# A four-layer transformer kernel: the first stage in another order, its normalising on ScalarE, and the row transfers of layer 0 spread between products

## The chip, the cores and the metric

The kernel runs on one core of one Trainium2 chip. The metric is the device time of one execution, in microseconds. Three runs of the kernel before gave 928.27, 928.96 and 929.91 us; the median, 928.96 us, is the time before.

## What is computed

The input x is 16 batches of 128 tokens of 128 numbers, in fp32; a context tensor has 2048 rows of the same width. Four layers follow, each of two residual updates, with a gate (a tanh of one number) on each:

```
x = x + tanh(g_xattn[l]) * attention_l(layernorm(x), ctx)
x = x + tanh(g_ffn[l])   * ffn_l(layernorm(x))
```

Layer 0's attention is linear: `scores = tril(ctx ctx^T)` and the output is `Q + scores Q` with Q the normalised tokens. Its feed-forward has 8 experts of 256 hidden units, of which each token uses two:

```python
logits = flat @ Wr
topk_vals, topk_idx = top_k(logits, 2)
topk_w = softmax(topk_vals)
combine = sum(one_hot(topk_idx, 8) * topk_w[..., None], axis=1)
for e in range(8):
    y = silu(flat @ Wg[e]) * (flat @ Wu[e]) @ Wd[e]
    out = out + y * combine[:, e:e + 1]
```

Layer 1 has softmax attention and 16 experts with grouped routing and two shared experts; layer 2 has 16-head attention and a slot-based feed-forward with a GRU; layer 3 has 16-head attention at two scales, and 32 experts with one shared. The change touches layer 0 and the beginning of layer 1.

## The kernel before

Tokens are worked on in four groups of four batches, 512 tokens each; `X[g]` holds group g, tokens by features, in SBUF throughout. The names: PE is TensorE (matmuls), DVE VectorE, ACT ScalarE, POOL GpSimd, SP SyncE, which issues most DMAs. Each engine, and each DMA queue, runs its instructions strictly in the order in which a tile scheduler put them; that order comes from the order in which the Python code emits them and from their dependencies. An instruction that waits holds up all that stand behind it on the same engine.

**First stage.** `load_group` (L117) loads x and the context of a group, `load_ffn` (L144) the expert weights into one buffer `wall`. SP issues group 0, some constants, group 1, all of layer 0's weights, groups 2 and 3, then tables of rows, columns and later weights (L173 to L196). ScalarE's queue fills `xd`, 2 MB in HBM, with zeros (L212 to L217). `linear_attention(g)` (L500) transposes the context, normalises x, makes the masked scores `sm`, multiplies (`po`), and updates X[g] (L518, L519). `normed` (L249) takes means and variances on DVE, one power on POOL (`rs`, L260), and scales on DVE (`xn`, L264), four instructions of 128x128. The driver (from L1122) emits group 0's linear attention, its routing, and then groups 1 to 3 in turn. `weights_0` (L522) picks the two greatest logits and takes a softmax with an exponential (L379).

**Layer 0's experts.** `experts()` (L1028) is a generator that the driver asks for one result after the other; attention and other work is emitted between. For group 0 all 16 half-experts are computed on all tokens. One of them, called a product here, is `gated` (L440) and `down`: gate product `pg` (L445), up product `pu` (L446), SiLU `sg` on ACT (L453; in layer 1 a tanh at L450 and a DVE product at L451), `h = sg*pu` on DVE (L457), `hw = h*cb` with the token's weight, on POOL or DVE (L461), and two products later the down product, summed in `acc` (L1036). `cb` is one expert's weights of 512 tokens on all partitions, broadcast from HBM by SP (`spread`, L428). For group 0 the products from 8 on have `hw` on DVE, the others on POOL; for layer 1's group 0 it is on DVE for the products before 12.

**Groups 1 to 3 by routing.** `choose_0` (L855) is advanced at group 0's products 0, 1, 2, 4, 6, 8 and 13: normalising groups 1 to 3 into `xs`, logits and weights of all three together, counting matmuls (`counts`, L873 to L876), row numbers `to` (L897). Then POOL scatters the rows of `xs` into `xd`, sorted by expert, with 24 indirect DMAs in a row (L901). The last step makes `whose`, the expert of each block of 128 rows, and `by`, the weights of rows. `blocks_0` (L930) computes the 31 blocks of `xd` by the expert they belong to (transposes L966, products L988, weight copies `wb` L982) and writes `yd`. In the middle stands `attention_1(0)`, layer 1's attention for group 0. `return_0` (L1008) fetches each token's two rows from `yd` with indirect DMAs on POOL (L1017, eight a group, 24 in all), and adds them to X[g] with eight adds on DVE (L1024). Its steps stand at the products 0 to 12 of layer 1's first group:

```python
if (layer, g) == (1, 0):
    for i in range(BYE, NG):
        back = return_0(i)
        for k, n in enumerate(((0, 0, 2), (3, 4, 7), (8, 9, 12))[i - BYE]):
            steps.setdefault(n, []).append(("x", back, (0, i) if k == 2 else None))
```

The next group's routing is advanced at the products 9, 11, 12 and 15 there.

Of the kernel before, what the change touches and what calls it, by code (L numbers as in the profile page):

```python
# [17 lines left out]
P = 128  # L18
# [41 lines left out]
def flamingo(ctx, tc, x_in, ctx_in, mask_in, w1, w2, w3, wslot, wsmall, slots, cols_in, rows_in, consts_in,  # L60
# [48 lines left out]


    def load(name, src, dtype=F32):
        t = const.tile(list(src.shape), dtype, tag=name, name=name)
        nc.sync.dma_start(t[:], src)
        return t
# [3 lines left out]
    def load_group(g):  # L118
        xg = const.tile([P, GB, D], F32, tag=f"x{g}", name=f"x{g}")
        nc.sync.dma_start(xg[:], x_in[g * GB:(g + 1) * GB].rearrange("b s d -> s b d"))  # L120
        X.append(xg)
        cg = act.tile([P, GB, D], F32, tag="oT" if g < 2 else "qT", name="cg")
        nc.sync.dma_start(cg[:], ctx_in[g * GB:(g + 1) * GB].rearrange("b s d -> s b d"))
        C.append(cg)
# [6 lines left out]
    def weights_by_head(name, src):  # L131

        t = blank(name, [P, 4, P])
        for n in range(2):
            for s in range(2):
                o = t[:, 2 * n + s, :].rearrange("p (i x) -> p i x", i=4)
                a = src[:, n * D + 64 * s:n * D + 64 * s + 64].rearrange("p (j i d) -> p j i d", j=2, i=4)
                for j in range(2):
                    nc.sync.dma_start(o[:, :, DK * j:DK * j + DK], a[:, j])
# [32 lines left out]

    load_group(0)  # L173
    gates = load("gates", rows_in[:, 0:8].to_broadcast([P, 8]))
    wsm = load("wsmall", wsmall)
    consts = load("consts", consts_in)
    WIDE = {0: 2, 1: 4, 3: 4}
    LOADS = {0: ("0", gu0, dn0, 16, 0), 1: ("1", gu1, dn1, 18, 2), 3: ("3", gu3, dn3, 17, 1)}
    FW = {}
    load_group(1)  # L180
    FW[0], parts = load_ffn(0)
    for part in parts:
        part()
    load_group(2)
    load_group(3)
    rows = load("rows", rows_in.to_broadcast([P, NROWS]))
    cols = load("cols", cols_in)
    at = dict(offsets(CONSTS))["up"][0]
    nc.sync.dma_start(consts[P // 2:, at:at + P], consts_in[:P // 2, at:at + P])
    W1 = load("w1", w1)  # L190
    mask_i = load("mask", mask_in, I32)
    WS = load("wslot", wslot)
    SL = load("slots", slots)
    WO3 = const.tile([P, 2, D], F32, tag="wo3", name="wo3")
    for u in range(2):
        nc.sync.dma_start(WO3[u * P // 2:(u + 1) * P // 2], w3[:, 3 * D:].rearrange("(s p) d -> p s d", s=2))  # L196

    ROW, CON = offsets(ROWS), offsets(CONSTS)

    def row(name):  # L200
        at, n = ROW[name]
        return rows[:, at:at + n]

    def col(name):
        i = COLS.index(name)
        return cols[:, i:i + 1]

    def con(name):
        at, n = CON[name]
        return consts[:, at:at + n]  # L210

    vp = blank("vp", [P, GB, VB])  # L212
    xd, yd = [dram.tile([NBLK * P, D], F32, tag=n, name=n, bufs=1) for n in ("xd", "yd")]
    zeros, z0 = vp[:].rearrange("p t x -> p (t x)"), xd[:].rearrange("(p r) d -> p (r d)", p=P)
    for i in range(0, NBLK * D, GB * VB):
        n = min(GB * VB, NBLK * D - i)
        nc.scalar.dma_start(z0[:, i:i + n], zeros[:, :n])  # L217

# [14 lines left out]
    nc.gpsimd.tensor_copy(count[:], counted[:])  # L233
    tgx = const.tile([P, 4], F32, tag="tgx", name="tgx")
# [14 lines left out]
    def normed(g, xn=None):  # L249
# [11 lines left out]
        if xn is None:  # L261
            xn = act.tile([P, GB, D], F32, tag=tag_of("xn"), name="xn", bufs=1)
        for t in range(GB):
            nc.vector.tensor_scalar(xn[:, t, :], x[:, t, :], mv[:, t, 0:1], rs[:, t:t + 1], ALU.subtract, ALU.mult)  # L264
# [75 lines left out]
    def first(v, n, k):  # L340
# [10 lines left out]
        sel = small.tile([P, nt, n], F32, tag=tag_of("sel"), name="sel", bufs=2 if side[0] == "x" else 1)  # L351
# [59 lines left out]
    def spread(comb, ne, width):  # L411
# [12 lines left out]
        for e in range(ne // n):  # L424
            cb = bcast.tile([P, GT], F32, tag="cb", name="cb")
            for i in range(n):
                k = P // n
                nc.sync.dma_start(cb[i * k:(i + 1) * k], by[i, e:e + 1].to_broadcast([k, GT]))  # L428
# [11 lines left out]
    def gated(chain, w, xnT, cb, tanh, banks, vector):  # L440
# [13 lines left out]
        if cb is None and tanh:  # L454
            nc.vector.scalar_tensor_tensor(h[:], sg[:], 0.5, pu[:], ALU.mult, ALU.mult)
        else:
            nc.vector.tensor_tensor(h[:], sg[:], pu[:], ALU.mult)  # L457
# [3 lines left out]
        (nc.vector if vector else nc.gpsimd).tensor_tensor(hw[:], h[:], cb[:], ALU.mult)  # L461
# [38 lines left out]
    def linear_attention(g):  # L500
        pt = tr_tile()
# [5 lines left out]
        xn = normed(g)  # L507
# [5 lines left out]
        nc.vector.tensor_tensor(sm[:], ps, bc(tri[:], 1, GB), ALU.mult)  # L513
        po = split(acc_tile())
        for t in range(GB):
            mm(po[:, t, :], sm[:, t, :], xn[:, t, :])
        y = work.tile([P, GB, D], F32, tag="se", name="y0")
        nc.vector.tensor_tensor(y[:], po, xn[:], ALU.add)  # L518
        add_gated(g, y[:], tgx[:, 0:1])  # L519


    def weights_0(p):  # L522
# [3 lines left out]
        sel, m8 = first(more, 8, 2)  # L526
        return sel, softmax_selected(l, m8[:, :, 0], sel, 8, "0")
# [306 lines left out]

    def with_tanh(layer, g):
# [3 lines left out]
    def routing(layer, g):  # L839

        xn = normed(g)
# [3 lines left out]
        comb = weights_0(logits_of(xnT, wsm[:, 0:8], 8))[1] if layer == 0 else weights_1(xnT) if layer == 1 else weights_3(xnT, with_tanh(layer, g))  # L845
# [9 lines left out]
    def choose_0():  # L855

        xs = act.tile([P, NT, D], F32, tag="kTm", name="xs", bufs=1)
        groups = range(BYE, NG)
        for i, g in enumerate(groups):
            normed(g, xs[:, i * GB:(i + 1) * GB])  # L860
            yield
        p = bank("logits")[:, :NT * 8].rearrange("p (t e) -> p t e", e=8)
        for i, g in enumerate(groups):
            xT = transposed(xs[:, i * GB:(i + 1) * GB], "a0", act, None)
            for t in range(GB):
                mm(p[:, i * GB + t, :], xT[:, t * P:(t + 1) * P], wsm[:, 0:8])
        yield
        sel, comb = weights_0(p)
# [8 lines left out]
        yield  # L877
# [19 lines left out]
        nc.vector.tensor_scalar(to[:], two[:, 0:2, :], -1.0, None, ALU.add)  # L897

        for t in range(NT):
            for k in range(2):  # L900
                apart("xd", nc.gpsimd.indirect_dma_start(  # L901
                    out=xd[:], out_offset=bass.IndirectOffsetOnAxis(ap=to[:, k, t:t + 1], axis=0), in_=xs[:, t, :],
                    in_offset=None))
        yield
# [18 lines left out]
        yield  # L923
# [84 lines left out]
    def return_0(g):  # L1008

        to, by, _ = places[0]  # L1010
        ys = []
        for k, tag in enumerate(("xns", "xnTs")):
            y = act.tile([P, GB, D], F32, tag=tag, name="y0", bufs=1)
            ys.append(y)
            for t in range(GB):
                i = (g - BYE) * GB + t
                apart(f"y{g}{k}", nc.gpsimd.indirect_dma_start(  # L1017
                    out=y[:, t, :], out_offset=None, in_=yd[:],
                    in_offset=bass.IndirectOffsetOnAxis(ap=to[:, k, i:i + 1], axis=0)))
            yield  # L1020
        for k, y in enumerate(ys):
            for t in range(GB):
                i = (g - BYE) * GB + t
                nc.vector.scalar_tensor_tensor(X[g][:, t, :], y[:, t, :], by[:, k, i:i + 1], X[g][:, t, :], ALU.mult,  # L1024
                                               ALU.add)
        yield

    def experts():  # L1028
# [23 lines left out]
        for at, (layer, g) in enumerate(ORDER):  # L1052
# [10 lines left out]
            if moving:  # L1063
                nxt = choose_0()
# [270 lines left out]
```

## Time and profile before

| | |
|---|---|
| median of three runs | 928.96 us |
| the profiled execution | 930.84 us |
| its span | 929.1 us |
| mean granted TensorE clock | 0.965 |
| busy: PE, DVE, ACT, POOL | 834.3, 580.6, 259.3, 282.6 us |
| `hw` on POOL, 128x512 | 126 times, mean 1278 ns |
| `h` on DVE, 128x512 | mean 683 ns |
| `xn` on DVE, 128x128 | mean 399 ns |
| gather on POOL | 24 times, mean 987 ns |

A row of a timeline or a group has the start, the busy time, the engine, the line, the operation, `out<-in` by the program's names, and in brackets how long the engine stood idle ahead of it and which instruction ended the wait ("issue" where the profile shows none). PEld is TensorE's weight load, which runs beside PE. A matmul in fp32 shows as two. The granted clock is the share of full speed at which TensorE was allowed to run. In the slices each digit is the busy share in tenths of one fortieth of the span. The profiled execution lasted 1.7 us longer than its span.

### The profile page before, as it was taken

What the parts mean: (1) busy time and instruction counts of PE and PEld (TensorE: products, weight loads), DVE (VectorE), ACT (ScalarE), POOL (GpSimd) and SP (SyncE); (2) the same over time, 40 slices, a digit from 0 to 9 for tenths busy, and PEclk for the clock granted to TensorE, in tenths of its full rate; (3) what the DMA queues carried; (4) which work ended last, traced back from release to release, by engine and by line L of the source; (5) the groups of instructions that cost most, each with busy time, mean ns of one, the idle gap of its engine ahead of it and who ended that gap; (6) DMA issues with size and microseconds to landing.
All of it is one profiled execution on the core that took longest, in us unless ns stands there. A gap on an engine that the chain in (4) does not pass through costs nothing.

```text
span 929.1 us, 16015 instructions
## 1 busy us (share of the span) xinstructions
PE 834.3 (90%) x6183; PEld 468.5 (50%) x6183; DVE 580.6 (62%) x1628; ACT 259.3 (28%) x457; POOL 282.6 (30%) x283
## 2 busy tenths in 40 slices
PE   3889399877999999999899999999989998999997
PEld 3554289534544554455455555555554554554443
DVE  4756252566977475666675866677666668566622
ACT  1222166221321222232223222223222232322321
POOL 3326521353233124311421113421114223313443
PEclk9979699978999999999999999999999999999999
DMA  9711212552121012100202112310002111211231
GB/s 305 211 17 40 64 46 79 159 162 63 24 69 44 27 35 80 46 21 28 69 35 67 35 47 62 123 37 24 24 24 72 35 48 46 76 51 49 94 103 34
DMA packets 55677, 62.12 MB, mean 67 GB/s; under 512 B 14312, under 2 KB 33512, under 8 KB 55472
## 3 DMA queue, kind: packets, MB, share of 16 engines
q1 hardware_dynamic: 53776, 55.90, 19.9%
q0 software_dynamic: 1536, 3.15, 1.1%
q10 hardware_dynamic: 288, 2.03, 0.6%
q8 instruction: 49, 0.80, 0.4%
q14 instruction: 28, 0.23, 0.1%
HBM read 53.97 MB, written 7.09 MB: 66 GB/s over the span
## 4 chain that ended last, share of the span: by engine, by line
PE 54%; DVE 21%; POOL 8%; issue 8%; ACT 4%; DMA 2%; another core or an unknown queue 1%; SPq 1%; POOLq 0%; DVEq 0%; ACTq 0%
PE mm L108 8%; PE acc L1036 7%; PE pg L445 7%; PE pu L446 7%; POOL hw L461 3%; DVE sg L451 3%; PE mm L593 2%; PE po L487 2%; DVE h L457 2%; DVE mp L481 2%; POOL rs L260 2%; POOL y L1017 2%; DVE xn L264 2%; PE tr L244 2%; PE po L490 2%
## 5 line engine op out<-in xcount | busy, mean ns | idle before, releaser
L461 POOL TENSOR_TENSOR hw<-h,cb 128x512 f32<-128x512 f32 x126 | 161.0, 1278 | 459.4 <-DVE h L457 348.1
L446 PE MATMUL pu<-xnTx,wall 128*128 128x512 f32 x288 | 156.4, 626 | 14.9 <-DVE sg L451 13.1
L1036 PE MATMUL acc<-hw,wall 128*128 128x512 f32 x288 | 153.9, 618 | 10.6 <-DVE h L457 9.9
L445 PE MATMUL pg<-xnTx,wall 128*128 128x512 f32 x288 | 154.8, 620 | 7.8 <-issue 4.7
L450 ACT ACTIVATE sg<-pg 128x512 f32<-128x512 f32 x123 | 73.6, 598 | 244.7 <-PE pg L445 230.5
L457 DVE TENSOR_TENSOR h<-sg,pu 128x512 f32<-128x512 f32 x145 | 99.1, 683 | 60.9 <-PE pu L446 40.7
L451 DVE SCALAR_TENSOR_TENSOR sg<-sg,pg 128x512 f32<-128x512 f32 x123 | 83.6, 680 | 51.4 <-ACT sg L450 51.3
L1036 PEld LDWEIGHTS acc<-hw,wall 128*128 128x128 f32 x288 | 55.1, 198 | 71.3 <-issue 53.0
L446 PEld LDWEIGHTS pu<-xnTx,wall 128*128 128x128 f32 x288 | 52.4, 197 | 75.9 <-issue 39.1
L481 DVE TENSOR_REDUCE mp<-mm 128x4 f32<-128x512 f32 (+1 forms) x112 | 65.8, 645 | 21.1 <-PE mm L593 19.9
L445 PEld LDWEIGHTS pg<-xnTx,wall 128*128 128x128 f32 x288 | 50.1, 194 | 50.2 <-issue 35.1
L495 DVE RECIPROCAL rcw<-po 128x128 f32<-128x128 f32 (+1 forms) x28 | 25.2, 900 | 57.1 <-PE po L490 44.8
L264 DVE TENSOR_SCALAR xn<-x,mv,rs 128x128 f32<-128x128 f32 x116 | 40.3, 399 | 25.4 <-POOL rs L260 25.4
L615 ACT ACTIVATE pts<-mm 128x512 f32<-128x512 f32 x64 | 33.6, 602 | 73.3 <-PE mm L609 73.3
L487 PE MATMUL po<-pts,vp 128*32 128x128 f32 (+1 forms) x896 | 46.1, 274 | 7.6 <-ACT pts L615 6.7
L260 POOL TENSOR_TENSOR rs<-ve,neghalf 128x4 f32<-128x4 f32 x32 | 33.2, 1037 | 61.8 <-DVE ve L258 61.7
L490 PE MATMUL po<-pts,own 128*32 128x128 f32 (+1 forms) x896 | 44.3, 266 | 0.5 <-issue 0.5
L453 ACT ACTIVATE sg<-pg 128x512 f32<-128x512 f32 x33 | 19.7, 597 | 67.9 <-PE pg L445 58.4
L487 PEld LDWEIGHTS po<-pts,vp 128*32 128x32 f32 (+1 forms) x896 | 21.3, 108 | 29.9 <-ACT pts L615 14.0
L254 DVE BATCH_NORM_STATS2 st<-x 128x6 f32<-128x128 f32 x128 | 29.5, 280 | 10.2 <-DMA x<-in_x 9.9
L593 PE MATMUL mm<-kTm,qT 32*128 32x256 f32 x256 | 30.5, 413 | 0.0
L1017 POOL DMA_INDIRECT y<-yd,to x24 | 23.7, 987 | 21.7 <-DMA yd<-yb 8.8
(335 smaller groups left out, 1226.0 us busy)
## 6 DMA issues: line engine op xcount, KB each, us to landing
cb<-combD SPq DMA_DIRECT2D x72, 256.0 KB
cb<-combD SPq DMA_DIRECT2D x128, 128.0 KB
wall<-in_gu SPq DMA_DIRECT2D x24, 256.0 KB
wall<-in_dn SPq DMA_DIRECT2D x12, 256.0 KB
xb<-xd SPq DMA_DIRECT2D x7, 256.0 KB
yd<-yb SPq DMA_DIRECT2D x7, 256.0 KB
xd<-vp ACTq DMA_DIRECT2D x1, 1072.0 KB
x<-in_x SPq DMA_DIRECT2D x4, 256.0 KB
```

The costliest lines, as they stand in the source:

```text
L108: nc.tensor.matmul(out=o, lhsT=l, rhs=r, start=start, stop=stop)
L264: nc.vector.tensor_scalar(xn[:, t, :], x[:, t, :], mv[:, t, 0:1], rs[:, t:t + 1], ALU.subtract, ALU.mult)
L445: in_turn(chain, nc.tensor.matmul(out=pg[:], lhsT=w[:, 0], rhs=xnT[:], start=True, stop=True))
L446: in_turn(chain, nc.tensor.matmul(out=pu[:], lhsT=w[:, 1], rhs=xnT[:], start=True, stop=True))
L450: nc.scalar.activation(sg[:], pg[:], AF.Tanh, scale=0.5)
L451: nc.vector.scalar_tensor_tensor(sg[:], sg[:], 1.0, pg[:], ALU.add, ALU.mult)
L457: nc.vector.tensor_tensor(h[:], sg[:], pu[:], ALU.mult)
L461: (nc.vector if vector else nc.gpsimd).tensor_tensor(hw[:], h[:], cb[:], ALU.mult)
L481: nc.vector.tensor_reduce(mp[:, 0:n, 32 * i + 16:32 * i + 18], src, AX.X, ALU.max)
L487: in_turn(chain, nc.tensor.matmul(out=po[32 * jj:32 * jj + 32, 0, :], lhsT=vcols, rhs=pts, start=first, stop=last, skip_group_check=True))
L490: in_turn(chain, nc.tensor.matmul(out=po[32 * jj:32 * jj + 32, 1, :], lhsT=own[rows, r, :], rhs=pts, start=False, stop=last, skip_group_ch ...
L1036: in_turn(chain, nc.tensor.matmul(out=acc[0][:], lhsT=w[:, 2], rhs=h[:], start=n == 0, stop=last))
```

## The change

The loads come in another order: context 0 on ScalarE's queue, all of x and the context ahead of most weights, the zero fill of `xd` behind them on SP's queue, and the tables of later layers behind the broadcasts of `cb`. The first stage is emitted by a list, `FIRST`, with the linear attention, group 0's routing ("r") and the choosing of groups 1 to 3 ("c1" to "c3") as generators. Layer 0 normalises on ScalarE. The sum `po + xn` is made by a matmul with the identity. The weights of the two chosen experts come from a tanh; logits and weights are made group by group, and `places_0` then counts over all. The scatters are spread over the products 6 to 15 (one or two each, the rest after the last), each behind the latest `hw` on POOL; the gathers over the products 0 to 17 of layer 1's group 0 and the first two of group 1, in turn from both lists, with two more buffers; the adds come at product 6 (group 1), 14 (group 2) and product 4 of the next group (group 3). In layer 0's group 0, `hw` is on DVE at the even products from 6 on, in layer 1's group 0 at those before 4. The next routing there is advanced at 12, 14, 15 and 17. `attention_1(0)` is emitted after group 0's experts end, as before, but TensorE's order now has its head (transposes to scores) ahead of the first block.

The diff, cut to its core:

```diff
-        nc.sync.dma_start(cg[:], ctx_in[g * GB:(g + 1) * GB].rearrange("b s d -> s b d"))
+        (nc.sync if g else nc.scalar).dma_start(cg[:], ctx_in[g * GB:(g + 1) * GB].rearrange("b s d -> s b d"))
...
+    load_group(1)
+    FW[0], parts = load_ffn(0)
+    parts[0]()
+    load_group(2)
+    load_group(3)
+    for part in parts[1:]:
+        part()
+    consts = load("consts", consts_in)
+    xd, yd = [dram.tile([NBLK * P, D], F32, tag=n, name=n, bufs=1) for n in ("xd", "yd")]
...
+        nc.sync.dma_start(z0[:, i:i + n], zeros[:, :n])
...
-        for t in range(GB):
-            nc.vector.tensor_scalar(xn[:, t, :], x[:, t, :], mv[:, t, 0:1], rs[:, t:t + 1], ALU.subtract, ALU.mult)
+        if on_act:
+            off = small.tile([P, GB], F32, tag="off", name="off")
+            nc.gpsimd.tensor_tensor(off[:], mv[:, :, 0], rs[:], ALU.mult)
+            nc.gpsimd.tensor_scalar(off[:], off[:], -1.0, None, ALU.mult)
+        for t in range(GB):
+            if on_act:
+                nc.scalar.activation(xn[:, t, :], x[:, t, :], AF.Identity, bias=off[:, t:t + 1], scale=rs[:, t:t + 1])
...
-        y = work.tile([P, GB, D], F32, tag="se", name="y0")
-        nc.vector.tensor_tensor(y[:], po, xn[:], ALU.add)
-        add_gated(g, y[:], tgx[:, 0:1])
+        in_turn(chain, nc.tensor.matmul(out=po, lhsT=ident[:], rhs=xn[:], start=True, stop=False, skip_group_check=True))
...
+        add_gated(g, po, tgx[:, 0:1])
...
-        return sel, softmax_selected(l, m8[:, :, 0], sel, 8, "0")
+        nc.vector.tensor_tensor(mid[:], m8[:, :, 0], m8[:, :, 1], ALU.add)
...
+        nc.scalar.activation(e[:], e[:], AF.Tanh)
...
+    SEND = [(n, 1 + (n + 1) % 2) for n in range(6, 16)]
+    FETCH = {0: [(n, 2) for n in range(4)] + [(n, 1) for n in range(4, 18)], 1: [(0, 1), (1, 1)]}
+    ADD = {0: [(6, 1), (14, 2)], 1: [(4, 3)]}
+
+    def on_vector(layer, g, n):
+
+        return (layer, g) == (0, BYE - 1) and n > 5 and n % 2 == 0 or (layer, g) == (1, 0) and n < 4
...
         for t in range(NT):
             for k in range(2):
-                apart("xd", nc.gpsimd.indirect_dma_start(
+                yield
+                ins = nc.gpsimd.indirect_dma_start(
                     out=xd[:], out_offset=bass.IndirectOffsetOnAxis(ap=to[:, k, t:t + 1], axis=0), in_=xs[:, t, :],
-                    in_offset=None))
-        yield
+                    in_offset=None)
+                apart("xd", ins)
+                behind_of("hw", ins)
...
+            tags = ("ya", "yb") if (g - BYE) % 2 else ("xns", "xnTs")
...
+                        if not t and not k:
+                            behind_of("h", ins)
...
+                    apart(f"y{g}{k}", ins)
+                    behind_of("hw", ins)
+                    yield
...
-                for n in (9, 11, 12, 15) if (layer, g) == (1, 0) else (3, 7, 8, 13):
+                for n in (12, 14, 15, 17) if (layer, g) == (1, 0) else (3, 7, 8, 13):
...
+    FIRST = [0, 0, 1, 0, 1, "r", 1, "r", 2, 2, "c1", "r", 2, "r", "c1", 3, 3, "c2", "c1", 3, "c2", "c3", "c2", "c3", "c3"]
...
+    first_of = {g: linear_attention(g) for g in range(NG)}
+    first_of["r"] = routing(0, 0)
+    first_of.update({f"c{g}": choose_0(g) for g in range(BYE, NG)})
+    for name in FIRST:
+        side[0] = "x" if name == "r" else "m"
+        next(first_of[name])
     side[0] = "m"
-    for g in range(1, NG):
-        linear_attention(g)
+    latest["spread"] = latest["cb"]
+    rows = load("rows", rows_in.to_broadcast([P, NROWS]))
...
+    sending, fetching = places_0(), return_0()
+    next(sending)
```

`behind_of("hw", ins)` orders an instruction behind the latest `hw` on POOL at that point of the emission, without a wait on another engine; `behind_of("spread", ins)` does so for the broadcasts of `cb`. The two softmax weights are written as half of one plus or minus the tanh of half their difference: `e = tanh(l - (top1 + top2)/2)`, then `0.5*e + 0.5`, times the selection.

## The prediction

> **What bounds the kernel now.** I read the page's slices first, then a table of windows, then the timelines of GpSimd and VectorE in the two stretches where TensorE stands still. In the slices (23.2 us each) TensorE is the bound nearly everywhere, but for the first slice, the fifth (93 to 116 us) and the eighth to tenth (163 to 232 us):
>
> ```profile
> PE   3889399877999999999899999999989998999997
> PEclk9979699978999999999999999999999999999999
> ```
>
> The windows give sizes. Columns: the stretch, its length, then busy time of PE, PEld, DVE, ACT and POOL with counts, the granted clock, the DMA share and GB/s.
>
> ```profile
> 90.00:100.00 10.00, 3.91 (x10) 1.41 (x8) 1.38 (x2) 0.60 (x1) 7.66 (x8) 0.95 0.16 52
> 100.00:110.00 10.00, 2.79 (x6) 1.23 (x7) 1.38 (x2) 0.58 (x1) 5.55 (x7) 0.50 0.21 63
> 112.00:170.00 58.00, 57.24 (x460) 54.10 (x461) 25.25 (x82) 32.86 (x61) 11.36 (x18) 0.97 0.21 59
> ...
> 180.00:184.00 4.00, 0.00 (x0) 0.00 (x0) 1.80 (x5) 0.60 (x1) 3.09 (x4) 1.00 0.54 193
> 184.00:200.00 16.00, 9.79 (x13) 3.61 (x14) 7.69 (x25) 0.60 (x1) 12.06 (x12) 0.61 0.70 208
> ...
> 213.00:217.60 4.60, 0.00 (x0) 0.00 (x0) 1.53 (x4) 0.13 (x1) 3.39 (x6) 0.71 0.20 53
> ...
> 226.00:287.00 61.00, 57.30 (x221) 30.49 (x220) 50.52 (x167) 18.54 (x32) 18.22 (x18) 1.00 0.17 50
> ```
>
> Between 112 and 170 TensorE is full, and after 226 nearly so; what is won at 90 to 110 or at 180 to 218 therefore passes on to the end. The cause of both holes is GpSimd's queue. First the scatters, 24 of them, one each 1.26 us (0.96 and 0.30 of issue), once the row numbers `to` are there (DVE line):
>
> ```profile
> 74.15 0.16 DVE L897 TENSOR_SCALAR to<-two 128x24 int32<-128x24 f32 x1
> ```
>
> ```profile
> 74.62 1.23 POOL L901 DMA_INDIRECT xd<-xs,to  x1 [1.72 <-DVE rank_in L915]
> 76.15 0.96 POOL L901 DMA_INDIRECT xd<-xs,to  x1 [0.30 <-issue]
> ...
> 103.93 0.95 POOL L901 DMA_INDIRECT xd<-xs,to  x1 [0.30 <-issue]
> 104.88 1.73 POOL L982 COPY wb<-wall 128x512 f32 x3
> 112.66 1.04 POOL L260 TENSOR_TENSOR rs<-ve,neghalf 128x4 f32<-128x4 f32 x1 [6.05 <-DVE ve L258]
> ```
>
> The blocks' first product starts at 111.92. Then the gathers of layer 1's first group, from 175.99 to 214, at the same 1.25 us. Behind each stands a VectorE add (L1024), and behind the adds in VectorE's own order the gating products `h`:
>
> ```profile
> 182.20 0.35 DVE L1024 SCALAR_TENSOR_TENSOR x<-y,by,x 128x128 f32<-128x128 f32 x1 [5.21 <-DMA y<-yd,to]
> ...
> 191.98 0.66 DVE L457 TENSOR_TENSOR h<-sg,pu 128x512 f32<-128x512 f32 x1
> ...
> 216.07 0.35 DVE L264 TENSOR_SCALAR xn<-x,mv,rs 128x128 f32<-128x128 f32 x1 [5.09 <-POOL rs L260]
> ```
>
> VectorE's `h` of product 3 is ready to run near 182 and runs at 191.98, since eight adds with late data stand ahead of it; `xn` waits at 216 for an `rs` that GpSimd holds behind eight gathers. From 170 to 287 TensorE idles 19.1 us (0.01, 4.00, 6.21, 0.51, 4.60, 0.06 and 3.70 by the windows), and the half clock after each hole costs some 5.9 more (9.79 busy x 0.39 lacking = 3.8, and from 217.6 to 226 8.34 x 0.25 = 2.1). That is all there is to win there, about 25 us.
>
> **Part by part, first stage.** Removed: the xd fill and constants ahead of the inputs, so x1 lands near 6 instead of 10.8 (VectorE's wait for it ended at 10.80) and group 1 is updated near 21.7 instead of 28.5; four adds of 0.69 us on VectorE; two exponential table loads of 1.28. Added: 4 matmuls with the identity (0.86 each warm), 16 normalising activations instead of VectorE's 0.34 each, two tiny GpSimd operations a group. No row shows a scalar activation of 128x128 with two pointers; a 128x256 exponential takes 0.384 and a 128x512 with a pointer bias 0.687, so I take 0.4 to 0.5 each, 1.65 for four against 1.1 on VectorE. ScalarE is 28% busy, so this lies under other work except in group 0's own chain, which also gets the two GpSimd operations: its normalised tokens come about 4 us later (26.8 against 22.7), but without the reduce, reciprocal and table load the first product is at about 32.5 against 30.51. If that cover fails the start is up to 2 us later still.
>
> The counting matmuls start at 67.14 now and `to` follows 7.0 later. In the new order they stand behind the products 4, not 7: three products fewer, 3 x 2.57 = 7.7, and the other groups' first stage is some 6.8 ahead. So 32.5 + (67.1 - 30.5) - 7.7 - 6.8 = 54.6, and `to` at about 62 (60 to 64). By then product 5's hw (1.28 by the row of 126, mean 1278) stands ahead of the scatters, so they begin near 64.
>
> **Scatters between products.** From there GpSimd's order holds 24 scatters x 1.26 = 30.3, five hw x 1.28 = 6.4, and two weight copies x 0.61 = 1.2: 37.9 together, ending near 102 against 104.9. Two products take TensorE 2 x 2.57 = 5.14, and GpSimd one hw and three scatters, 1.28 + 3.78 = 5.06: neither waits long for the other. TensorE ends group 0's products near 88, and ten scatters remain behind. In the new order attention 1's head for group 0 comes ahead of the first block, and its `rs` stands behind the last scatter: 102 + 1.0 (rs) + 1.1 (xn) + 1.05 (transposes) + 0.6 (copy) = 105.7, then two projections at half clock 3.8, 0.7 for the bias copy, two warm 2.1, values and scores 2.0, block transposes and copy 1.7: first block product near 116. Before it is at 111.92, but the head's 6.65 us (transposes from 115.08, projections to scores from 117.29 to 122.89) and 1.2 of half clock come later, so the same point is 119.8. Gain 4. It can be 9 if `to` comes at 58, and -4 if it comes near 70. Two long unexplained waits lie under the train now (ScalarE 7.72 before 97.44, VectorE 9.80 before 102.34). If such waits fall between products in the new order, they cost 0 to 8; I take 0, since ten scatters still end last.
>
> Here a rule speaks against the change. The Trainium skill, "SBUF — State Buffer", section "A bandwidth-pool intuition that's wrong (but worth ruling out)", says that a GpSimd-issued DMA that takes about 620 ns alone takes about 3100 ns while VectorE holds the shared port. The row says otherwise: the scatters take 0.96 both from 80 to 92, with VectorE's products running, and from 93 to 102, with VectorE idle. By the row the 14 scatters that now lie between products cost nothing more; by the rule each waits at least for one 0.68 us product, 14 x 0.68 = 9.5, and the stage gains -5.5 instead of 4. I take the row, since those products are the same instructions.
>
> **Gathers between products.** Now 8 gathers in one run and all eight adds ahead of `h` of product 3. In the new order eight gathers still lead, but group 1's adds are taken singly between the products 2 and 6, and each further gather has a hw of product n in front of it. GpSimd then needs 1.28 + 1.26 = 2.54 per product, TensorE 2.57. Landing 5 us after issue as now, `h` of product 3 runs near 184, of 4 near 187, of 5 near 191.4, of 6 near 197 (208.85 now). VectorE loses eight hw of 0.68 to GpSimd, which is where the slack comes from; what is late next is GpSimd itself, with `rs` (1.05) and the row add (1.26) between hw and gather. Walking on to the scores of attention 1, group 1, the same counts of products put them at 209.3 instead of 221.2: gain 11 or 12, I take 11. Bounds: 5 if the `rs` still waits for a full train, 18 if nearly all the idle and cold time of 25 goes. Routing of layer 1's next group ends three products later, with its broadcasts issued at the last product. The row for this is the stage's own start at 170, where routing also ended last and TensorE was busy 9.99 of 10 us: I take 0, with 3 as the other end. Later loads (layers 2 and 3) are moved behind the broadcasts into a time with a DMA share of 0.2: nothing.
>
> **Sum.** 930.84 for the profiled execution (span 929.1, 1.7 around it), less 4 and 11: 915.8. The median of the three runs, 928.96, lies 1.9 under the profiled one: 914.0.
>
> **The rivals.**
> - A, as above: 914, own range 908 to 921. For it: both holes follow one queue, and the rates of GpSimd and TensorE match. Chance 0.52.
> - B, nearly all stalls go: stage one gains 9 (`to` at 58), stage two 18: 902. For it: the idle and cold time is there. Against: GpSimd has no slack at 2.54 of 2.57. Chance 0.17.
> - C, GpSimd stays the bound: stage one gains nothing, as hw and weight copies stretch the train by 7.6 and eat the earlier start, and the gathers gain 5: 924. For it: GpSimd carries more work in both stages. Chance 0.17.
> - D, slower: the scatter train in GpSimd's in-order queue. It is 37.9 long instead of 30.3, so all rests on an earlier `to`. It decides at `to` near 66: later than that, the stage loses. If the reordered first stage gains nothing (`to` at 74.15), the train ends at 114, the stage loses 8, the gathers give 5 back: 932. For it: group 0's first product starts later, and three routings of 12 small VectorE operations replace one. Against: counts stand three products earlier in TensorE's order. Chance 0.14. That the change does nothing is not likely: the order of all five engines differs.
>
> About 0.2% (1.9 us) is what a measurement of this kernel can tell from no change. Faster by more: A, B and most of C, 0.82; within: a part of C, 0.04; slower: D, 0.14. The range takes in B and C, from 901 to 928; D and gains over 28 stay out.
>
> **What would show it.** `to` at 60 to 64 with scatters ending near 102, each still 0.96; the first block product near 116, with attention 1's head before it; no hole at 180 to 184 or 213 to 217 (less 4 us); `h` of product 3 within 2 us of its up-projection. Wrong would be: scatters or gathers over 1.3 us in length beside VectorE's products, `to` after 66, GpSimd full and TensorE waiting for hw from product 4 on in layer 1, or a new wait at the start of layer 1's second group.

## The result, and the profile after

The changed kernel takes 922.61 us (median of 5 runs, 919.22 to 924.82) against 928.96: a ratio of 0.9931, 95% interval 0.9905 to 0.9956. That is 6 us faster where 15 was forecast. Measured again, on another chip, it was 921.37 against 930.46, 9 us, a ratio of 0.9909 (0.9883 to 0.9936). The profiled execution, 919.22 us with a span of 917.5, is the fastest of the five; times inside it are read for where stalls lie, not for a us of the total.

TensorE's slices on the page:

```profile
PE   5897599889879999999999999999989999999997
```

The fifth slice still has a hole (5 for 3), the ninth and tenth are fuller (8 and 9 for 7 and 7), but the eleventh fell from 9 to 8 and the twelfth from 9 to 7. The row numbers and the scatters, from the timelines of VectorE and GpSimd:

```profile
56.65 0.16 DVE L935 TENSOR_SCALAR to<-two 128x24 int32<-128x24 f32 x1
```

```profile
59.51 1.28 POOL L941 DMA_INDIRECT xd<-xs,to  x1 [0.19 <-DMA w2h<-in_w]
...
64.21 1.27 POOL L470 TENSOR_TENSOR hw<-h,cb 128x512 f32<-128x512 f32 x1 [1.98 <-DVE h L462]
65.63 1.01 POOL L941 DMA_INDIRECT xd<-xs,to  x1 [0.15 <-issue]
...
98.32 0.97 POOL L941 DMA_INDIRECT xd<-xs,to  x1 [0.31 <-issue]
99.31 1.06 POOL L257 TENSOR_TENSOR rs<-ve,neghalf 128x4 f32<-128x4 f32 x1
```

TensorE's timeline has the hole behind the scatters, and the first block product:

```profile
101.17 1.15 PE L241 MATMUL tr<-ident,xn 128*128 128x128 f32 x4 [11.77 <-DVE xn L268]
...
111.33 1.16 PE L1034 MATMUL pg<-xbT,wb 128*128 128x128 f32 x8 [0.68 <-ACT xbT L1014]
```

The row numbers come 17.5 us earlier, the scatters end 5.6 earlier, and the first block product starts 0.6 earlier, with attention 1's head for group 0 already done. The first gather then starts at 166.18, 9.8 us before 175.99. From there on hardly anything more is gained. A point that both kernels share is the copy of the last expert sum of layer 1's second group, from which on TensorE's order is all but the same in both. Before, and then after:

```profile
369.33 0.59 ACT L1039 COPY yT<-acc 128x512 f32<-128x512 f32 x1 [1.16 <-PE acc L1036]
```

```profile
359.03 0.58 ACT L1092 COPY yT<-acc 128x512 f32<-128x512 f32 x1 [1.16 <-PE acc L1089]
```

That is 10.3 us earlier, where the first gather was 9.8 earlier.

How that comes about is seen when both are cut into stretches of 50 us from the first gather. First the kernel before:

```profile
176.00:226.00 50.00, 34.62 (x89) 15.83 (x88) 27.78 (x76) 10.01 (x15) 29.00 (x31) 0.80 0.46 135
226.00:276.00 50.00, 46.98 (x192) 25.89 (x192) 41.96 (x146) 15.38 (x27) 14.11 (x14) 1.00 0.18 53
276.00:326.00 50.00, 47.52 (x438) 23.96 (x436) 30.16 (x56) 11.26 (x21) 9.85 (x8) 1.00 0.11 34
```

The changed kernel:

```profile
166.20:216.20 50.00, 41.64 (x119) 19.56 (x118) 28.43 (x74) 11.90 (x19) 29.70 (x29) 0.90 0.48 148
216.20:266.20 50.00, 41.36 (x138) 20.28 (x138) 38.00 (x123) 12.23 (x21) 22.89 (x23) 0.97 0.16 50
266.20:316.20 50.00, 46.40 (x277) 24.01 (x275) 40.24 (x112) 11.42 (x21) 17.06 (x17) 1.00 0.14 43
```

TensorE's busy time (first column after the length) rises by 7.0 us in the first stretch, falls by 5.6 in the second and by 1.1 in the third. The clock, 0.80 to 0.90 and 1.00 to 0.97, says the same. The gain of the first stretch is given back 50 us later. Where, VectorE's timeline shows:

```profile
190.10 0.68 DVE L462 TENSOR_TENSOR h<-sg,pu 128x512 f32<-128x512 f32 x1
191.20 0.50 DVE L1064 SCALAR_TENSOR_TENSOR x<-y,by,x 128x128 f32<-128x128 f32 x1 [0.41 <-DMA y<-yd,to]
...
196.38 0.35 DVE L1064 SCALAR_TENSOR_TENSOR x<-y,by,x 128x128 f32<-128x128 f32 x1 [3.29 <-DMA y<-yd,to]
...
200.22 0.35 DVE L1064 SCALAR_TENSOR_TENSOR x<-y,by,x 128x128 f32<-128x128 f32 x1 [2.95 <-DMA y<-yd,to]
...
225.53 0.67 DVE L462 TENSOR_TENSOR h<-sg,pu 128x512 f32<-128x512 f32 x1
226.12 0.34 DVE L1064 SCALAR_TENSOR_TENSOR x<-y,by,x 128x128 f32<-128x128 f32 x1
...
250.10 0.35 DVE L1064 SCALAR_TENSOR_TENSOR x<-y,by,x 128x128 f32<-128x128 f32 x1 [2.26 <-DMA y<-yd,to]
...
254.45 0.35 DVE L1064 SCALAR_TENSOR_TENSOR x<-y,by,x 128x128 f32<-128x128 f32 x1 [1.47 <-DMA y<-yd,to]
254.72 0.68 DVE L578 TENSOR_TENSOR aT<-po,qT 128x512 f32<-128x512 f32 x1
```

The adds at 191.20, 196.38, 200.22, 250.10 and 254.45 each wait for a row, and VectorE's other work stands behind them. TensorE's own timeline has the holes that follow, 3.16 us behind `sg` after the add at 200.22 and 4.74 behind `aT` after the one at 254.45:

```profile
204.53 1.80 PE L451 MATMUL pu<-xnTx,wall 128*128 128x512 f32 x2 [3.16 <-DVE sg L456]
...
255.45 1.57 PE L108 MATMUL mm<-w,aT 128*128 128x128 f32 x8 [4.74 <-DVE aT L578]
```

From 60 to 300 us, VectorE's waits for rows are 19.8 us in ten, against 9.7 in three before. The last gather starts at 248.86, where before it was 214.01.

These adds do not stand where the change meant them. Of each group's eight adds only the first is ordered behind the latest `h` (in the kernel, `if not t and not k: behind_of("h", ins)`), and the second follows it, since both update the same tokens. For group 2 these two ran at 226.12 and 226.50, behind `h` of product 14 (225.53), as meant. The six others ran from 191.20 to 221.81, the first of them right behind `h` of product 7 (190.10). Of the 19.8 us of waits 16.3 fall on such adds of groups 2 and 3.

### The profile page after: what moved, and what is told of

The parts are those of the page before. It is cut to its first block, busy times and chain, and to the rows that moved or that the text cites. A ratio compares the mean times of both kernels' runs of the same rounds, so it can differ in the third digit from the quotient of the medians.

```text
span 917.5 us, 16089 instructions
## 1 busy us (share of the span) xinstructions
PE 831.0 (91%) x6191; PEld 464.1 (51%) x6191; DVE 571.5 (62%) x1598; ACT 266.3 (29%) x484; POOL 302.0 (33%) x312
## 4 chain that ended last, share of the span: by engine, by line
PE 48%; DVE 20%; POOL 13%; issue 9%; DMA 5%; ACT 4%; POOLq 0%; SPq 0%; DVEq 0%; ACTq 0%
PE mm L108 8%; POOL hw L470 6%; PE acc L1089 6%; PE pg L450 6%; PE pu L451 5%; DVE mp L490 3%; DVE sg L456 3%; PE mm L617 2%; PE po L496 2%; POOL xd L941 2%; DVE h L462 2%; DMA y<-yd,to 2%; POOL rs L257 2%; PE po L499 2%; PE mm L612 2%
## 5 line engine op out<-in xcount | busy, mean ns | idle before, releaser
L470 POOL TENSOR_TENSOR hw<-h,cb 128x512 f32<-128x512 f32 x137 | 176.2, 1287 | 443.5 <-DVE h L462 353.7
L451 PE MATMUL pu<-xnTx,wall 128*128 128x512 f32 x288 | 154.4, 618 | 10.5 <-DVE sg L456 9.0
L451 PEld LDWEIGHTS pu<-xnTx,wall 128*128 128x128 f32 x288 | 51.9, 194 | 72.5 <-issue 39.8
L268 DVE TENSOR_SCALAR xn<-x,mv,rs 128x128 f32<-128x128 f32 x96 | 33.1, 402 | 24.1 <-POOL rs L257 24.1
L241 PE MATMUL tr<-ident,xn 128*128 128x128 f32 x100 | 22.4, 310 | 19.2 <-DVE xn L268 17.0
L496 PEld LDWEIGHTS po<-pts,vp 128*32 128x32 f32 (+1 forms) x896 | 21.4, 108 | 30.3 <-ACT pts L639 14.8
L241 PEld LDWEIGHTS tr<-ident,xn 128*128 128x128 f32 x100 | 12.6, 142 | 35.9 <-issue 14.6
```

Of the source, the lines that this page charges most:

```text
L451: in_turn(chain, nc.tensor.matmul(out=pu[:], lhsT=w[:, 1], rhs=xnT[:], start=True, stop=True))
L470: latest["hw"] = nc.gpsimd.tensor_tensor(hw[:], h[:], cb[:], ALU.mult).ins
L496: in_turn(chain, nc.tensor.matmul(out=po[32 * jj:32 * jj + 32, 0, :], lhsT=vcols, rhs=pts, start=first, stop=last, skip_group_check=True))
```

## The experiments

Times are medians, ratios are against the kernel before on the same chip. Where two experiments ran on different chips, a difference of 1 or 2 us between them says little. The changed kernel itself once more, on the chip on which three of the others ran (no adds, plain first stage, scatters in one run with the gathers of before):

> The changed kernel as it is, beside the other three on one chip. Both theories: within 2 us of its first measurement, 920 to 925; it is the base for the three others of this call.

921.37 us, ratio 0.9909 (0.9883 to 0.9936). As expected.

**Which part gained.** The gathers put back as before, in the changed kernel:

```diff
-        return (layer, g) == (0, BYE - 1) and n > 5 and n % 2 == 0 or (layer, g) == (1, 0) and n < 4
+        return (layer, g) == (0, BYE - 1) and n > 5 and n % 2 == 0 or (layer, g) == (1, 0) and n < 12
...
-                for n in (12, 14, 15, 17) if (layer, g) == (1, 0) else (3, 7, 8, 13):
+                for n in (9, 11, 12, 15) if (layer, g) == (1, 0) else (3, 7, 8, 13):
...
-                for n, k in FETCH.get(g, ()):
-                    steps.setdefault(n, []).extend([("x", fetching, None)] * k)
...
+                    back = return_0(i)
+                    for k, n in enumerate(((0, 0, 2), (3, 4, 7), (8, 9, 12))[i - BYE]):
```

(and `return_0` as it was)

> The changed kernel with layer 0's gathers, adds, weightings and routing steps in layer 1's first group put back as before: only the first stage and the scatters are changed. Theory (the first stage and scatters give all, the spread gathers give nothing): first gather near 166, as in the changed kernel, and 921 to 925 us, no slower than the changed kernel by over 2. Rival (the gathers gave part of it and something later took it): 926 to 929.

920.32 us, ratio 0.9913 (0.9881 to 0.9946), first gather at 168.12. With the adds in place, the first stage and the scatters give all of the gain. The mirror, the kernel before with only that part changed:

> The kernel before with only the gathers, adds, weightings and routing steps of layer 1's first group spread as in the change. Theory: 927 to 931 us, no gain, since each add waits in VectorE's queue for a row that a weighting on GpSimd holds back. Rival (my forecast of 11 us for this part): 916 to 920.

931.95 us, ratio 1.0032 (1.0012 to 1.0052). My 11 us for this part are refuted; alone it costs 3.

**The first stage.** Scatters in one run:

```diff
-    SEND = [(n, 1 + (n + 1) % 2) for n in range(6, 16)]
+    SEND = [(6, 2 * NT)]
...
-        return (layer, g) == (0, BYE - 1) and n > 5 and n % 2 == 0 or (layer, g) == (1, 0) and n < 4
+        return (layer, g) == (0, BYE - 1) and n > 5 or (layer, g) == (1, 0) and n < 4
...
-                behind_of("hw", ins)
```

> The changed kernel, but all 24 scatters in one run after product 6 and the weightings of all products after 5 on VectorE: GpSimd has nothing between the scatters. Theory (the earlier row numbers are what gained; the spreading only lengthens the train, 37.9 instead of 30.3 us): the last scatter near 90 instead of 99, first block product near 102 instead of 111, and 912 to 916 us. Rival (spreading the scatters is what gains, because a run of scatters holds TensorE up): 925 or more.

915.18 us, ratio 0.9857 (0.9829 to 0.9884), 6 to 7 us faster than the changed kernel. GpSimd's and TensorE's timelines of this run:

```profile
58.76 1.22 POOL L941 DMA_INDIRECT xd<-xs,to  x1 [4.17 <-DVE to L935]
...
89.74 0.96 POOL L941 DMA_INDIRECT xd<-xs,to  x1 [0.30 <-issue]
```

```profile
94.92 1.11 PE L1011 MATMUL tr<-ident,xb 128*128 128x128 f32 x4 [6.53 <-DMA xb<-xd]
96.71 2.08 PE L1033 MATMUL pg<-xbT,wb 128*128 128x128 f32 x8 [0.68 <-ACT xbT L1013]
```

The last scatter starts at 89.74 instead of 98.32, since only one weighting (at 61.42) still stands among the scatters. TensorE ends group 0's products at about the same time as in the changed kernel, and its hole is 6.53 us instead of 11.77. The first block comes even before the 102 expected, since in this order it stands ahead of attention 1's head. So of the change's two ideas for the scatters, row numbers early is the one that gains, and spreading them between weightings takes a part of it away. What the other place of attention 1's head adds was not tried apart. Normalising back on VectorE:

```diff
-        normed(g, xs[:, own], on_act=True)
+        normed(g, xs[:, own])
```

(and the same in `routing` and `linear_attention`)

> The changed kernel with layer 0's normalising back on VectorE, everything else as changed. Theory (the order of the first stage gained, and the move to ScalarE is nearly neutral, since group 0's own chain gets longer by two GpSimd operations and a slower scale): row numbers within 2 us of 58 and 920 to 925 us. Rival (ScalarE's share is what brings the row numbers forward): row numbers after 62 and 926 or more.

924.05 us, ratio 0.9955 (0.9936 to 0.9974), row numbers at 58.93. The traces that keep the changed kernel's first stage up to there have them at 56.65 to 58.51, so ScalarE brings them forward by 2 us at most. Of the time it gives some 1 to 4 us, hardly clear of noise, as the intervals overlap. And the list `FIRST` in a plain order:

```diff
-    FIRST = [0, 0, 1, 0, 1, "r", 1, "r", 2, 2, "c1", "r", 2, "r", "c1", 3, 3, "c2", "c1", 3, "c2", "c3", "c2", "c3", "c3"]
+    FIRST = [0] * 3 + ["r"] * 4 + [1] * 3 + [2] * 3 + [3] * 3 + ["c1"] * 3 + ["c2"] * 3 + ["c3"] * 3
```

> The changed kernel with its hand-written order of the first stage put back to a plain one: group 0's linear attention and routing, then the groups 1, 2, 3, then their choices; loads, ScalarE's normalising and the tanh weights stay. Theory (the earlier row numbers come from the counts standing three products earlier and from the loads, not from the interleaving): row numbers at 55 to 61, within 3 us of the changed kernel. Rival (the interleaving is what gains): row numbers after 64 and 926 or more.

924.28 us, ratio 0.9947 (0.9924 to 0.997), row numbers at 59.64, 1.4 later than in the changed kernel on the same chip (58.20). So most of the 17.5 us by which the row numbers come earlier are left even in the plain order, and the time is 2.9 us more than the changed kernel's, as the theory had it. Whether the loads or the counts' place in TensorE's order bring them was not tried apart.

**What holds the second half.** The 24 adds left out of the changed kernel (groups 1 to 3 then lack layer 0's experts):

```diff
-                for t in range(GB):
+                for t in range(0):
                     for k, y in enumerate(ys):
                         ins = nc.vector.scalar_tensor_tensor(X[g][:, t, :], y[:, t, :], by[:, k, t0 + t:t0 + t + 1],
```

> The changed kernel with the 24 adds of the fetched rows left out; the gathers stay, but nothing reads their rows, so groups 1 to 3 go on without layer 0's experts. Theory (late rows ahead of VectorE's other work are what TensorE still waits for in layer 1's first group): the 20 us of waits and 8 us of adds leave VectorE, and 905 to 913 us. Rival (that stretch is held by VectorE's and GpSimd's other work, weightings, routing and norms, and the rows only decide where the holes lie): 917 to 922.

901.66 us, ratio 0.9704 (0.9674 to 0.9734), 19.7 less than the changed kernel on the same chip and more than expected. The 50 us from its first gather on:

```profile
168.20:218.20 50.00, 49.21 (x158) 23.65 (x157) 35.96 (x82) 16.07 (x25) 37.28 (x36) 1.00 0.50 157
```

With the same gathers and weightings on GpSimd, which is even busier (37.28 us against 29.70), TensorE is full at 49.21 of 50. GpSimd's pace was not the bound; the adds were. The run takes away three things together: VectorE's waits for rows, the adds' own 8 us, and the wait of attention 1 for their sums. The kernel before with its adds left out in the same way:

> The kernel before with the 24 adds of the fetched rows left out, gathers as they were, so groups 1 to 3 go on without layer 0's experts. Theory (the return of the rows costs the same in both kernels, the change only moves its stalls): some 20 us less than before, 907 to 912, as with the changed kernel. Rival (the change did shorten the return, and something else took the gain): 25 us or more less, under 905.

920.67 us, ratio 0.9901 (0.9866 to 0.9937): only 8.3 less. Neither number of the expectation holds; the adds cost much more in the changed kernel. What is left before without adds is one large hole in TensorE's timeline:

```profile
208.12 1.02 PE L108 MATMUL tr<-cols,perm 128*128 128x4 f32 x4 [12.34 <-POOL perm L1165]
```

`perm` is made on GpSimd behind the train of gathers. So spreading the gathers does take this block away: without adds the two kernels are 18 to 19 us apart (ratios 0.9704 and 0.9901, medians 901.66 and 920.67), of which the first stage is about 8, and 10 to 11 are left for the spread gathers (with the weightings and the routing that moved with them), about what was forecast. With the adds, which cost 8.3 before and 19.7 after, they are gone.

Adds later, each behind the latest `h`:

```diff
-    ADD = {0: [(6, 1), (14, 2)], 1: [(4, 3)]}
+    ADD = {0: [(8, 1), (16, 2)], 1: [(5, 3)]}
...
-                        if not t and not k:
-                            behind_of("h", ins)
+                        behind_of("h", ins)
```

> The changed kernel with the three sets of adds two products later, the last one product later (8, 16 and 5 instead of 6, 14 and 4), and each add ordered behind the latest h, so that their rows have landed. Theory (single adds with late rows in VectorE's queue took the gain): waits of adds for rows fall from 14 us to under 5, and 915 to 919 us. Rival (GpSimd itself, with a weighting ahead of every gather, is the bound): 921 to 925.

918.89 us, ratio 0.9896 (0.9864 to 0.9928). With every add held to its product, the waits for rows are gone altogether. Yet only 1 to 4 us are won, not 20, and the intervals overlap, so late rows alone are not what the adds cost. TensorE has other holes now, among them 4.39 us at 237.50 for `comb`, the routing of the next group. Eight adds, 231.39 to 235.87, now stand within its chain of small operations on VectorE. Hence two runs with the routing put forward again, as before the change:

```diff
-                for n in (12, 14, 15, 17) if (layer, g) == (1, 0) else (3, 7, 8, 13):
+                for n in (9, 11, 12, 15) if (layer, g) == (1, 0) else (3, 7, 8, 13):
```

in the changed kernel,

> The changed kernel with one number list put back: the next group's routing in layer 1's first group is advanced at the products 9, 11, 12 and 15 instead of 12, 14, 15 and 17. Theory (in the changed kernel the second half of layer 1's first group is held by group 3's late rows, not by the routing): within 2 us of the changed kernel, 920 to 925. Rival (the later routing gave the gain back): 915 to 918.

928.69 us, ratio 1.0015 (1.0001 to 1.0029), and with the later adds,

> The kernel with the later adds, and with the routing at the products 9, 11, 12 and 15 as before. Theory (with the rows' waits gone, the late routing is what TensorE waits for next, 4.4 us before the transpose of comb): that wait goes, and 912 to 917 us against 918.9 without. Rival (VectorE's chain is the bound whatever its order): 918 to 921.

927.1 us, ratio 0.9984 (0.9963 to 1.0005). Both expectations and both rivals were wrong: an earlier routing costs 6 to 10 us (928.69 against 921.37 to 922.61, or by the ratios 1.0015 against 0.9909 to 0.9931; 927.1 against 918.89), and with the later adds the wait for `comb` stays (3.82 at 241.03). From the first gather to the copy of the shared point it takes 200.2 and 200.6 us instead of 192.9. With the rows spread over 80 us, the late routing is not a price of the change but a need. The rows fetched in one run and asked for late:

```diff
-    FETCH = {0: [(n, 2) for n in range(4)] + [(n, 1) for n in range(4, 18)], 1: [(0, 1), (1, 1)]}
-    ADD = {0: [(6, 1), (14, 2)], 1: [(4, 3)]}
+    FETCH = {0: [(0, 16), (8, 8)]}
+    ADD = {0: [(7, 1), (12, 2), (16, 3)]}
...
-        return (layer, g) == (0, BYE - 1) and n > 5 and n % 2 == 0 or (layer, g) == (1, 0) and n < 4
+        return (layer, g) == (0, BYE - 1) and n > 5 and n % 2 == 0 or (layer, g) == (1, 0) and n < 12
...
-                        if not t and not k:
-                            behind_of("h", ins)
+                        behind_of("h", ins)
...
-                    behind_of("hw", ins)
```

> The changed kernel with gathers in one run from the start of layer 1's first group (16, then 8 when buffers are free), not behind any weighting, the weightings of its products before 12 on VectorE, and the adds at the products 7, 12 and 16, each behind the latest h: rows come early and are asked for late. Theory (the pace of the weightings makes group 3's rows late, and VectorE waits for them): last gather before 212 instead of 249, no wait for rows, 910 to 916 us. Rival (VectorE with twelve weightings more than it can hide): 919 to 924.

921.91 us, ratio 0.9927 (0.9898 to 0.9956). The last gather starts at 198.84, the adds wait 0.3 us for rows in all, and nothing is won. GpSimd's timeline of this run, and TensorE's, show what is late in their place:

```profile
193.96 0.94 POOL L1071 DMA_INDIRECT y<-yd,to  x1 [0.30 <-issue]
194.92 1.04 POOL L257 TENSOR_TENSOR rs<-ve,neghalf 128x4 f32<-128x4 f32 x1
```

```profile
196.40 0.48 PE L241 MATMUL tr<-ident,xn 128*128 128x128 f32 x1 [5.61 <-DVE xn L268]
...
252.40 0.38 PE L421 MATMUL tr<-ident,comb 128*16 128x128 f32 x1 [4.92 <-DVE comb L378]
```

The `rs` of attention 1 stands behind the gathers again, as in the kernel before, and `comb` comes late out of VectorE's chain. So neither side of the expectation holds: it is not late rows alone, and not VectorE's weightings alone.

**Together.** Four combinations with the scatters in one run, each with edits shown above. With adds later and routing earlier:

> Three edits together: scatters in one run with the weightings of the products after 5 on VectorE, adds later and each behind the latest h, routing at 9, 11, 12 and 15. If the two stages are independent, the gains add: 7 from the scatters, 3 to 8 from the others, 907 to 912 us. If the first stage's gain is partly taken back in the second, as the changed kernel's was not by this one: 913 to 916.

914.85 us, ratio 0.9875 (0.9845 to 0.9905), no better than the scatters' edit alone (nor does it settle whether the stages add, since the earlier routing has its own cost). With the gathers as before:

> Scatters in one run with the weightings of the products after 5 on VectorE, and gathers, adds, weightings and routing of layer 1's first group as before. Theory (spread gathers neither gain nor lose): 913 to 917 us, as with spread gathers, 915.2. Rival (spread gathers gain some us once the first stage is short): 918 to 921.

917.36 us, ratio 0.9868 (0.9843 to 0.9892): as with spread gathers (0.9857), the intervals overlap. With the rows early and the adds late:

> The same with the scatters in one run and the weightings after product 5 of layer 0 on VectorE. If the two stages are independent, 6 us less than the kernel with rows early and adds late alone, 904 to 910 if that gained, 913 to 918 if not.

914.41 us, ratio 0.9844 (0.9816 to 0.9873), 7.5 less than without the scatters' edit: that edit's gain adds on. Finally adds later with the routing left late:

> Scatters in one run with the weightings after product 5 of layer 0 on VectorE, and the later adds (products 8, 16 and 5), routing as changed. If the gains of the two edits add: 6 to 7 less than the kernel with the later adds (918.9), 911 to 913 us. If the second stage gives the later adds' gain back: 914 to 916, as with the scatters' edit alone.

909.26 us, ratio 0.9776 (0.9753 to 0.98), 13 us faster than the changed kernel as first measured. It is the best of the versions that keep the adds, 2 us better than the lower case expected.

## Why the prediction was wrong

The sign was right, and the mechanism of the first stage. The total, 15, was more than twice the 6 us measured first (9 in the second measurement), and the split between the stages was nearly the reverse: 4 and 11 forecast, about 8 to 10 and 0 measured.

**First stage, 4 forecast.** `to` was put at 62 and came at 56.65: the first product ran at 31.50 instead of 32.5, the counts at 51.07 instead of 54.6, and `to` followed 5.6 later instead of 7.0. The train was put at 37.9 and took 39.8 (59.51 to 99.31), so its end was 99.3, not 102. From there to the first block product I allowed 14 us and it took 12.0. In these two terms the sum was off by 2.7 and 2.0, and with them the first block product is at 111.33 instead of 116. The point of before that I compared with, 119.8, was put together by hand; the next point that both kernels share in full, the first gather, is 9.8 us earlier. What I had as rival B's share for this stage, 9, was the right size. GpSimd kept pace with TensorE, as the rates 5.06 and 5.14 said, but that the train would still be shorter without the weightings, I had in my sum (30.3 against 37.9) and did not follow: it is probably most of the 6 to 7 us of the scatters' edit. The 16 normalising activations of the sum were 32 in the kernel, since routing and choosing normalise too.

The rule on the shared port did not bear on this case. The passage is about a `tensor_copy` on VectorE, and VectorE's products under the scatters are `tensor_tensor`, so the -5.5 worked out from it had no ground. The tile views of `xd`, of before and then of the changed kernel (minimum, median and maximum in ns):

```profile
L901 POOL DMA_INDIRECT xd<-xs,to x24: 954/958/1226, 74.6 to 103.9; - x24
```

```profile
L941 POOL DMA_INDIRECT xd<-xs,to x24: 954/969/1277, 59.5 to 98.3; - x24
```

The row was the right one: 11 ns more at the median, not 680.

The two unexplained waits under the train, taken at 0, did not come back as holes of that size: TensorE's last group-0 sums ran at 86.71, against 88 in the sum. Nor do they count in the old first stage: in the two other traces that have it, the last of these sums ran at 95.0 and 95.4 instead of 104.8, and the first block at 112.7 all the same.

**Second stage, 11 forecast: the step that failed** is "Walking on to the scores of attention 1, group 1, the same counts of products put them at 209.3 instead of 221.2: gain 11 or 12". The walk has group 1's adds in it and puts those of groups 2 and 3 at nothing, without a reason. To product 6 it holds: shifted by the 9.8 us of the first stage, `h` of the products 3, 4 and 5 ran at 185.2, 187.8 and 191.6, where I put 184, 187 and 191.4, and `h` of product 6 at 194.5, even before my 197. Behind product 7 stand six adds of group 2, and the waits of the first three, 6.65 us together, hold VectorE. The point compared, the transpose of the attention's weights, before and then after:

```profile
221.24 0.87 PE L298 MATMUL tr<-ident,sm 128*128 128x128 f32 x4
```

```profile
207.83 0.81 PE L302 MATMUL tr<-ident,sm 128*128 128x128 f32 x4
```

Shifted, 207.83 is 217.6, 8.3 later than the 209.3 forecast: a gain of 3.6, not 11 or 12. Nor are the counts of products the same there: TensorE has begun nine before and eleven after. Two products are some 5.1 us of its time, so that by my estimate about 8.7 us were in hand at this point. Then I let the gain pass on to the end, because TensorE was nearly full after 226 before the change. But before, all rows had been fetched by 214. In the changed kernel the rows of groups 2 and 3 come until 249, VectorE waits for them, and the 7.0 us of the first 50 us are taken back by 5.6 and 1.1 in the next hundred. I had named as late next "GpSimd itself"; the run without adds, with TensorE busy 49.21 of 50 us while GpSimd did more, shows that it was not.

**What binds now.** The return of the rows runs through three orders: the rows' arrival ahead of VectorE's work, the `rs` and `perm` behind the gathers on GpSimd, and the routing chain on VectorE. Without adds the spread gathers are worth the 10 to 11 us worked out above; with adds one of the three is late in each order whose timelines are shown, and the stage from the first gather to the shared point took 190.5 to 200.6 us in all runs of the study that kept the adds, 193.3 before and 192.9 after. Which part of the 19.7 us that the adds cost is VectorE's time, which late rows and which the wait for their sums is not shown. That the spread gathers cost 3 us in the old kernel and none beside the new first stage was not followed further; nor why later adds gain 1 to 4 alone and 6 to 8 beside the scatters in one run. The earlier routing's 6 to 10 us are measured, and their course through VectorE's chain is not shown.

**The routing, taken at 0 with 3 at the other end**, has the other sign: beside spread gathers a late routing gains, since an early one costs 6 to 10.

## What to carry to other kernels

A gain in one stretch of a full engine is only a gain if what was moved out of that stretch finds room: walk on to the last instruction that was moved, and compare both kernels at a point where the orders are the same again. If an in-order queue is to feed another one, look at both ends: spreading the producer to free its queue makes the data late, and the consumer then waits in a queue with everything else behind it. Leaving the consumer out (here 24 small adds) tells in one run whether it is the consumer's end, though not which of its waits. And an order that is meant for a whole set of instructions has to be given to each of them: here two of each eight were held to their place, and group 2's other six ran up to seven products early.

## What the runs showed of the hardware

Not expected was how far runs of one kernel lie apart, and that the granted clock goes with it: the five runs of the best version gave 914.55, 910.74, 909.26, 908.99 and 906.42 us at mean clocks of 0.971, 0.977, 0.976, 0.977 and 0.980. Its profiled execution was the slowest of them, that of the changed kernel the fastest of five, so a difference of a few us between two profiles says little here, and medians of five or more were needed. A scalar activation of 128x128 with a pointer for scale and one for bias took 478 ns (32 of them, 477 to 493), the upper half of what was taken from the nearest rows.
